# Layer 0 alone: stores issued by ScalarE, x by group in one transfer, and six rows in the first chunk of values

## The chip, the cores and the metric

The kernel runs on one core of a Trainium2 chip. Its time is the device time in microseconds (us) of that core from the start to the end of the program. A core has a matrix engine (TensorE, PE in the profile), a vector engine (VectorE, DVE), an activation engine (ScalarE, ACT), a general engine (GpSimd, POOL) and an engine that only issues transfers (SyncE, SP). Each runs its own instructions in order, and they wait for each other through semaphores. Transfers between the main memory (DRAM) and the on-chip memory are moved by 16 DMA engines. They are started by an instruction on SP or ACT, and that engine goes on to its next instruction when the transfer has been issued, not when it has landed.

## The reference

Two layers run over x, 8 images of 256 channels and 64 x 64 pixels. Each has the form x + f(norm(x)), with a group norm over 8 neighbouring channels.

```python
# layer 0: a kernel of 3 x 3 taps made from the pixel itself (32 groups of 8 channels share it)
x1, x2, x3 = conv1x1(x, w1, b1), conv1x1(x, w2, b2), conv1x1(x, w3, b3)
h = concat([x1, unfold3(reflect_pad(x2))])
h = conv1x1(relu(bn(h)), cw1)
w = conv1x1(relu(bn(h)), cw2, cb2)           # (B, 32 groups, 9 taps, H, W)
out = einsum('bgskhw,bgkhw->bgshw', unfold3(zero_pad(x3)), w)
x = x + out
# layer 1: 7 x 7 window attention in 4 heads plus a dynamic depthwise convolution
q, k, v = c1x1(x, Wq), c1x1(x, Wk), c1x1(x, Wv)
att = softmax(q . (unfold7(reflect_pad(k)) + unfold7(pe)))
out_att = att . unfold7(reflect_pad(v))
out_conv = sum over taps of softmax(Wfc x) * dwconv(relu(dwconv(x)))
x = x + rate1 * out_att + rate2 * out_conv
```

## The kernel before

An image is cut into 8 bands of 8 rows (512 pixels), so there are 64 bands. Layer 0 runs ahead of layer 1 by 12 bands (`AHEAD = NB + 4`), and both are written into one loop over `g` from -12 to 63. The loop body has 8 steps `s`. Band `g` is done in layer 1, and the parts of layer 0 for the bands `g + 12`, `g + 11` and `g + 10` are put beside it by `beside` and `steer`. For `g < 0` there is no layer 1 yet: that stage is called alone in the code (`alone = g < 0`; for the tap weights and for the load of x by group it is `g < -1` and `g < -2`). The order on each engine is the order in which the program is written. `after(n, f)` puts a piece of work n places later, where `advance` counts six places for each step.

The parts of layer 0 for one band, in the order of their data:

- `load_x` (L99) brings x of a band in the layout channels by pixels twice, as `xs` for the statistics (L283) of an image that comes later and as `xc` for the convolutions.
- `small_maps` (L328) and `write_maps` (L343, L347) make x1 and x2, `value_maps` makes x3 in two halves of 128 channels (L369 on PE, L374 on ACT). Each half lies in `x3n` and is stored to DRAM by SP (L375), since the next part needs another layout.
- `hidden_maps` makes the hidden maps: L420 three times on ACT, L430 on PE, L437 on ACT. `tap_weights` makes the nine tap weights in three parts (L466 on PE).
- `values_by_group` loads `x3q`, x3 of a band in a layout with 32 groups times 4 quarters of the band in the partitions and 8 channels times 2 rows in each (L389, L393, L397: six transfers, and the last takes a row of the band after). `x_by_group` loads x of the band in the same layout, `xg`, as four transfers of a quarter each (L405). A run of memory in such a transfer is 2 rows of one channel, 128 elements or 512 bytes.
- `product(j)` multiplies a tap weight with x3q (L479 on DVE, 9 for a band). Alone, six of the nine products are added to xg on POOL (L487), and three are added up on PE (L500) and joined at the end on DVE (L507). `take` then makes the statistics for layer 1 (L515) and stores the band to DRAM as x1 with four transfers by SP (L519).

Layer 1 loads rows from x1 (`load_rows`, L553 to L557) and normalises them (L562). `values` makes the attention's values in chunks of 8 rows: chunk 0 of an image has the rows 3 to 7 of `yp` (its first three rows lie outside the image), the last chunk has four, and each of the others has 8. A matmul makes two rows (L592), and ACT copies them to `vc` (L600, L603). `store_values` stores a chunk to `vd` in DRAM, with three columns mirrored on each side: two transfers for the rows (L616) and, where the numbers of even and odd rows are equal, six for the mirrored columns (L621). Chunk 0 has five rows, so there the mirrored columns take twelve (L625). `mirror_rows` (L632) copies the mirrored rows, and `value_tile` loads what a tile of pixels needs (L643).

Two more orders matter. The framework gives the transfers of both issuing engines eight completion semaphores in turn, in the order of the program, so a transfer's issue also waits for the completion of the one eight before it. And buffers are in rings: `xs` has 1, `xc` 2, `xg` 3 (alone), `x3q` 2, `prod` 2, `x3n` one for each half and `vc` 1.

## Time and profile before

| | us |
|---|---|
| median of 3 runs | 3959.33 (3959.31 to 3961.93) |
| the profiled execution | 3964.1 |
| its span in the trace | 3962.3 |
| TensorE busy in it | 3794.8 |
| SP from the first to the last issue of the first chunk's edge columns (L625, 12 issues) | 7.92 |
| DMA share of queue q1 over the span (SP's transfers) | 44.9% of 16 engines |

The profiled execution is one run on its own. A difference that is worked out from its trace is taken from its own time first. In lines of the profile, `x<-x3n` is the store of x3, `x<-xg` the store of x1, `DVE L507` the addition that completes a band of layer 0 while it runs alone, and `SPq` an issue on SP, whose duration is that of the issue. A time line's row has the start, the duration, the engine, the line, the operation, output and input, and in brackets how long the engine had been idle and what ended that.

The page's 40 slices, of 99 us each, show the two stages: the first two and a half slices are layer 0 alone.

```profile
PE   5789999999999999999999999999999999999998
...
DMA  8874444544445444454445544444444544323211
```

### The profile page before, as it was taken

The numbers are of one execution on the slowest core, as the hardware profiler recorded it, in microseconds if no ns is written. First come the engines' busy times: TensorE is split into PE (matmuls) and PEld (weight loads), VectorE is DVE, ScalarE is ACT, GpSimd is POOL, SyncE is SP. The second block draws the span as 40 slices with busy tenths as digits, with TensorE's granted clock in tenths as the row PEclk, the third lists the DMA queues.
The fourth block names the chain that finished last, engine by engine and source line by source line (L and its number), as shares of the span: only waits on it lengthen the run. The fifth ranks groups of instructions, "written<-read, shape, count | busy, mean of one in ns | idle before, by whom it ended". The sixth has DMA issues, their size and how long they took to land.

```text
span 3962.3 us, 71885 instructions
## 1 busy us (share of the span) xinstructions
PE 3794.8 (96%) x24620; PEld 2110.4 (53%) x24620; DVE 3418.4 (86%) x7143; ACT 2839.8 (72%) x6779; POOL 3174.4 (80%) x2156
## 2 busy tenths in 40 slices
PE   5789999999999999999999999999999999999998
PEld 2345555555555555555555555555555555555554
DVE  5768988888988988888988988988988889978778
ACT  3457777777777777777777777777777777677776
POOL 4758988888987988978888888978988888966665
PEclk9999999999999999999999999999999999999999
DMA  8874444544445444454445544444444544323211
GB/s 227 194 184 115 123 119 114 134 125 123 119 109 144 123 122 109 118 142 125 119 111 129 131 123 122 111 135 127 117 112 104 127 116 107 86 69 92 71 60 34
DMA packets 489711, 472.80 MB, mean 119 GB/s; under 512 B 64208, under 2 KB 390400, under 8 KB 489088
## 3 DMA queue, kind: packets, MB, share of 16 engines
q1 hardware_dynamic: 486016, 463.66, 44.9%
q8 instruction: 194, 3.18, 0.3%
q10 hardware_dynamic: 3328, 4.55, 0.3%
q14 instruction: 173, 1.42, 0.1%
HBM read 329.08 MB, written 142.43 MB: 119 GB/s over the span
## 4 chain that ended last, share of the span: by engine, by line
PE 33%; POOL 26%; DVE 19%; ACT 9%; issue 6%; DMA 4%; SPq 3%; POOLq 0%; DVEq 0%; ACTq 0%
PE pf L872 15%; POOL xg L487 13%; POOL ex L1081 6%; DVE prod L479 4%; DVE rec L893 4%; DVE acc L855 4%; PE small L785 3%; ACT x L343 3%; PE sco L736 3%; PE ptp L773 2%; PE pq L671 2%; PE pk L692 2%; ACT ex L877 2%; POOL tot L888 2%; PE pv L592 2%
## 5 line engine op out<-in xcount | busy, mean ns | idle before, releaser
L872 PE MATMUL pf<-yp,c_wfc 128*128 128x512 f32 x4096 | 1909.2, 595 | 17.3 <-ACT ex L877 15.0
L487 POOL TENSOR_TENSOR xg<-xg,prod 128x1024 f32<-128x1024 f32 x549 | 1200.6, 2187 | 145.4 <-DVE prod L479 108.8
L872 PEld LDWEIGHTS pf<-yp,c_wfc 128*128 128x128 f32 x4096 | 740.2, 190 | 742.0 <-issue 644.0
L1081 POOL TENSOR_TENSOR ex<-ex,ex 128x1024 f32<-128x1024 f32 x384 | 907.8, 2364 | 53.9 <-ACT ex L877 49.8
L479 DVE SCALAR_TENSOR_TENSOR prod<-pw,c_par,x3q 128x1040 f32<-128x1040 f32 x576 | 737.5, 1287 | 137.1 <-PE pw L466 66.2
L829 DVE SCALAR_TENSOR_TENSOR acc<-yp,c_chan,acc 128x504 f32<-128x504 f32 (+3 forms) x1104 | 774.7, 702 | 41.0 <-ACT acc L820 20.6
L855 DVE SCALAR_TENSOR_TENSOR acc<-hid,c_chan,acc 128x504 f32<-128x504 f32 (+3 forms) x1024 | 749.4, 732 | 20.1 <-ACT acc L849 1.9
L877 ACT ACTIVATE ex<-pf 128x512 f32<-128x512 f32 x1024 | 602.4, 588 | 199.7 <-PE pf L872 184.7
L758 ACT ACTIVATE prob<-prob,nmax 128x196 f32<-128x196 f32 x1024 | 459.1, 451 | 210.7 <-DVE nmax L750 210.4
L767 ACT ACTIVATE prob<-prob,tot 128x196 f32<-128x196 f32 x1024 | 413.0, 452 | 231.4 <-DVE tot L765 230.5
L894 POOL TENSOR_TENSOR tot<-tot,rec 128x256 f32<-128x256 f32 x254 | 185.3, 729 | 402.7 <-DVE rec L893 386.1
L893 DVE RECIPROCAL rec<-tot 128x256 f32<-128x256 f32 x256 | 445.8, 1741 | 10.6 <-POOL tot L888 5.2
L775 ACT COPY pt<-ptp 112x512 f32<-112x512 f32 x511 | 294.8, 577 | 114.7 <-PE ptp L773 113.6
L750 DVE CUSTOM_DVE_ANT_0 prob<-sco,c_mask 128x196 f32<-128x196 f32 x1024 | 324.2, 354 | 22.1 <-PE sco L736 22.0
L773 PEld LDWEIGHTS ptp<-ident,prob 128*112 128x112 f32 x2044 | 226.3, 133 | 188.6 <-issue 136.2
L773 PE MATMUL ptp<-ident,prob 128*112 128x128 f32 x2044 | 320.4, 279 | 1.3 <-ACT vc L600 1.3
L785 PEld LDWEIGHTS small<-pt,vt 112*64 112x64 f32 x8144 | 258.8, 138 | 79.1 <-issue 75.7
L785 PE MATMUL small<-pt,vt 112*64 112x64 f32 x8144 | 295.1, 225 | 2.1 <-DMA vt<-vd 1.7
L736 PE MATMUL sco<-kb,qb 64*64 64x196 f32 x4096 | 235.9, 343 | 35.5 <-DVE kb L707 32.7
L592 PE MATMUL pv<-c_wv,yp 128*128 128x256 f32 (+1 forms) x1056 | 253.8, 383 | 7.2 <-ACT yp L562 6.0
L369 PE MATMUL p<-xc,w3s 128*128 128x512 f32 x512 | 247.6, 607 | 7.0 <-ACT ex L877 7.0
L888 POOL TENSOR_SCALAR tot<-tot 128x512 f32<-128x512 f32 x127 | 243.6, 1918 | 11.1
(139 smaller groups left out, 4689.5 us busy)
## 6 DMA issues: line engine op xcount, KB each, us to landing
vt<-vd SPq DMA_DIRECT2D x512, 112.0 KB
x<-x3n SPq DMA_DIRECT2D x128, 264.0 KB
x3q<-x SPq DMA_DIRECT2D x128, 264.0 KB
xc<-in_x SPq DMA_DIRECT2D x64, 512.0 KB
xg<-in_x SPq DMA_DIRECT2D x256, 128.0 KB
x<-xg SPq DMA_DIRECT2D x256, 128.0 KB
yp<-x SPq DMA_DIRECT2D x128, 256.0 KB
xr<-x SPq DMA_DIRECT2D x64, 512.0 KB
```

Source lines behind the costliest of these rows:

```text
L479: nc.vector.scalar_tensor_tensor(prod[:, :, :RUN], pw[:, j, :RUN].unsqueeze(1).to_broadcast([P, SHARE, RUN]), par[:, PCB2 + k : PCB2 + k + 1],
L487: nc.gpsimd.tensor_add(im.xg[i], im.xg[i], rows(prod))
L758: nc.scalar.activation(prob[:, h, :NKEY], prob[:, h, :NKEY], AF.Exp, bias=nmax[:, h : h + 1], scale=-1.0, accum_out=tot[:, h : h + 1],)
L767: nc.scalar.activation(prob[:, h, :NKEY], prob[:, h, :NKEY], AF.Copy, scale=tot[:, h : h + 1])
L773: nc.tensor.transpose(ptp[:, h, ch], prob[:, h, ch * CHUNK : (ch + 1) * CHUNK], ident)
L785: nc.tensor.matmul(po[half[h], :, t * TQ : (t + 1) * TQ], im.vt[i + ch, m][:n, t, (2 * ct + h) * HD : (2 * ct + h + 1) * HD], pt[:n, h, ch ...
L829: nc.vector.scalar_tensor_tensor(o, yp[:, ct, ra + dr : rb + dr, ca + dc : cb + dc], chan[:, ct, CW1 + k : CW1 + k + 1], o, ALU.mult, ALU.add,
L855: nc.vector.scalar_tensor_tensor(o, hid[:, ra + dr : rb + dr, ca + dc : cb + dc], chan[:, ct, CW2 + k : CW2 + k + 1], o, ALU.mult, ALU.add,)
L872: nc.tensor.matmul(pf, wfc[:, kt, 2 * m + j, ct * P : (ct + 1) * P], images[b].yp[i][:, kt, PAD : PAD + R], start=(kt == 0), stop=(kt == N ...
L877: nc.scalar.activation(ex[:, j].rearrange("p (r c) -> p r c", r=R), pf, AF.Exp)
L893: nc.vector.reciprocal(rec, v)
L1081: after(4, lambda ex=ex, exb=exb: nc.gpsimd.tensor_add(ex, ex, exb))
```

## The change

Three things are changed.

While layer 0 is alone, `value_maps` has its store of x3 issued by ScalarE, and `take` has the four stores of x1 issued by ScalarE nine places later (`keep`). Beside layer 1 both stay with SP.

The host lays out x a second time, by image and band in the layout of `xg`, so that a partition's 8 channels times 2 rows are one run of 1024 elements. `x_by_group` loads it with one transfer in place of four, for all 64 bands.

The first chunk of values has six rows, 3 to 8, in place of five. Row 8 is also the first row of the chunk after it. The numbers of even and odd rows are then equal in every chunk, so `store_values` has one form with six transfers for the mirrored columns, `values` one form with whole matmuls of two rows, and `vd` one row more.

```diff
-    def value_maps(b, i, mt):
+    def value_maps(b, i, mt, alone):
...
-        nc.sync.dma_start(out=im.x3[i][mt * P : (mt + 1) * P], in_=x3n[mt])
+        queue = nc.scalar if alone else nc.sync
+        queue.dma_start(out=im.x3[i][mt * P : (mt + 1) * P], in_=x3n[mt])
...
-        for q in range(NQR):
-            nc.sync.dma_start(
-                out=t[q * REL : (q + 1) * REL].rearrange("p s r c -> p s (r c)"), in_=pieces(x_in[b][:, i * BAND : (i + 1) * BAND], q)
-            )
+        nc.sync.dma_start(out=t.rearrange("p s r c -> p (s r c)"), in_=ins["xg"][b, i])
...
-            t = im.x1[i] = dram.tile([C, BAND], F32, tag="x1", name=f"x1_{b}_{i}")
+            im.x1[i] = dram.tile([C, BAND], F32, tag="x1", name=f"x1_{b}_{i}")
+            if alone:
+                after(9, lambda: keep(nc.scalar))
+            else:
+                keep(nc.sync)
+
+        def keep(queue):
             for q in range(NQR):
-                v = x[q * REL : (q + 1) * REL].rearrange("p s r c -> p s (r c)")
-                nc.sync.dma_start(out=pieces(t, q), in_=v)
+                v = im.xg[i][q * REL : (q + 1) * REL].rearrange("p s r c -> p s (r c)")
+                queue.dma_start(out=pieces(im.x1[i], q), in_=v)
...
-        first, last = (PAD, R) if j == 0 else (0, R) if j < NB else (R - 1, R + PAD)
+        first, last = (PAD, R + 1) if j == 0 else (0, R) if j < NB else (R - 1, R + PAD)
...
-            n = min(2, last - r) * W
-            if n <= 0:
+            if r >= last:
                 break
...
-                    pv[:n, g], yp[:, kt, r : r + n // W].rearrange("p r c -> p (r c)"), wv[:, kt],
+                    pv[:, g], yp[:, kt, r : r + 2].rearrange("p r c -> p (r c)"), wv[:, kt],
...
-        vd = im.vd[j] = dram.tile([R, WP, C], F32, tag="v", name=f"vd_{b}_{j}")
+        vd = im.vd[j] = dram.tile([R + 1, WP, C], F32, tag="v", name=f"vd_{b}_{j}")
...
-        count = [(last - first + 1 - p) // 2 for p in range(2)]
+        count = (last - first) // 2
...
-                if count[0] == count[1]:
-                    o = vd[at : at + 2 * count[0], to].rearrange("(u p) n -> p u n", p=2)
-                    nc.sync.dma_start(out=o, in_=vc[c : c + W + 1 : W, : count[0]])
-                else:
-                    for p in range(2):
-                        o = vd[at + p : at + p + 2 * count[p] - 1 : 2, to : to + 1].rearrange("u c n -> c u n")
-                        nc.sync.dma_start(out=o, in_=vc[p * W + c : p * W + c + 1, : count[p]])
+                o = vd[at : at + 2 * count, to].rearrange("(u p) n -> p u n", p=2)
+                nc.sync.dma_start(out=o, in_=vc[c : c + W + 1 : W, :count])
...
+    quarters = arr["x"].reshape(-1, REL, SHARE, NB, NQR, PIECE)
+    arr["xg"] = quarters.transpose(0, 3, 4, 1, 2, 5).reshape(-1, NB, P, SHARE * PIECE)
```

More of the change, by code (lines that the diff above doesn't have):

```diff
@@ L584, in values @@
         pv = ps.tile([P, 2, C], F32, tag="gen", name=f"pv_{b}_{j}_{half}", bufs=4)
-        done = []
         for g in range(2):
             r = first + 4 * half + 2 * g
-            n = min(2, last - r) * W
-            if n <= 0:
+            if r >= last:
                 break
@@ L592, in values @@
                 nc.tensor.matmul(
-                    pv[:n, g], yp[:, kt, r : r + n // W].rearrange("p r c -> p (r c)"), wv[:, kt],
+                    pv[:, g], yp[:, kt, r : r + 2].rearrange("p r c -> p (r c)"), wv[:, kt],
                     start=(kt == 0), stop=(kt == NCT - 1),
                 )
-            done.append(n)
+            n = g + 1
         def take():
-            if len(set(done)) == 1:
-                nc.scalar.copy(vc[: done[0], 2 * half : 2 * half + len(done)], pv[: done[0], : len(done)])
-            else:
-                for g, n in enumerate(done):
-                    nc.scalar.copy(vc[:n, 2 * half + g], pv[:n, g])
+            nc.scalar.copy(vc[:, 2 * half : 2 * half + n], pv[:, :n])
         return take
@@ L610, in store_values @@
         vc = im.vc[j]
-        vd = im.vd[j] = dram.tile([R, WP, C], F32, tag="v", name=f"vd_{b}_{j}")
+        vd = im.vd[j] = dram.tile([R + 1, WP, C], F32, tag="v", name=f"vd_{b}_{j}")
         first, last, at = value_rows(j)
-        count = [(last - first + 1 - p) // 2 for p in range(2)]
+        count = (last - first) // 2
         for p in range(2):
-            to = vd[at + p : at + p + 2 * count[p] - 1 : 2, PAD : PAD + W]
-            nc.sync.dma_start(out=to.rearrange("u c n -> c u n"), in_=vc[p * W : (p + 1) * W, : count[p]])
+            to = vd[at + p : at + p + 2 * count - 1 : 2, PAD : PAD + W]
+            nc.sync.dma_start(out=to.rearrange("u c n -> c u n"), in_=vc[p * W : (p + 1) * W, :count])
         for d in range(1, PAD + 1):
             for to, c in ((PAD - d, d), (PAD + W - 1 + d, W - 1 - d)):
-                if count[0] == count[1]:
-                    o = vd[at : at + 2 * count[0], to].rearrange("(u p) n -> p u n", p=2)
-                    nc.sync.dma_start(out=o, in_=vc[c : c + W + 1 : W, : count[0]])
-                else:
-                    for p in range(2):
-                        o = vd[at + p : at + p + 2 * count[p] - 1 : 2, to : to + 1].rearrange("u c n -> c u n")
-                        nc.sync.dma_start(out=o, in_=vc[p * W + c : p * W + c + 1, : count[p]])
+                o = vd[at : at + 2 * count, to].rearrange("(u p) n -> p u n", p=2)
+                nc.sync.dma_start(out=o, in_=vc[c : c + W + 1 : W, :count])
     def mirror_rows(b, j):
@@ L965, in beside @@
             if s == (2 if alone else 0):
-                (mid if alone else end).append(lambda: value_maps(bq_, iq, 0))
+                (mid if alone else end).append(lambda: value_maps(bq_, iq, 0, alone))
             if s == (3 if alone else 1):
-                mid.append(lambda: value_maps(bq_, iq, 1))
+                mid.append(lambda: value_maps(bq_, iq, 1, alone))
         if 0 <= g + AHEAD - 1 < B * NB and s == (2 if alone else 1):
```

## Prediction

> **What bounds the kernel now.** I read the page's busy times and 40 slices first, then a table of stretches, then the chain of waits of one short window, then each engine's own time line in that window.

> ```profile
> PE 3794.8 (96%) x24620; PEld 2110.4 (53%) x24620; DVE 3418.4 (86%) x7143; ACT 2839.8 (72%) x6779; POOL 3174.4 (80%) x2156
> ```

> ```profile
> 71.00:228.00 157.00, 122.69 (x591) 59.95 (x589) 125.06 (x140) 63.91 (x119) 114.14 (x88) 0.91 0.85 197
> 228.00:300.00 72.00, 60.10 (x301) 32.90 (x302) 44.61 (x93) 40.82 (x90) 37.51 (x22) 0.91 0.67 165
> 300.00:3900.00 3600.00, 3525.26 (x23204) 1972.09 (x23203) 3164.96 (x6734) 2670.13 (x6417) 2965.62 (x1995) 1.00 0.44 114
> ```

> In the table (stretch, its length, busy us of PE, PEld, DVE, ACT, POOL, TensorE clock, DMA share, GB/s) PE is busy 97.9% of 300 to 3900 us. That stage is TensorE's; a transfer that gets cheaper there is worth nothing. From 71 to 228 us, layer 0 alone, no engine is full: DVE 80%, PE 78%, POOL 73%, ACT 41%, the DMA engines 85%. What holds it is a chain. One band (from one L507, the addition that completes a band, to the next) reads:

> ```profile
> 129.10 1.22 DVE xg L507
> ...
> 132.28 0.61 SPq L519
> ...
> 133.64 0.43 SPq L375
> ...
> 136.22 0.61 SPq L405
> ...
> 139.47 6.39 DMA x3q<-x
> ...
> 145.98 0.15 DVE prod L479
> ...
> 147.79 1.09 DVE xg L507
> ```

> The time lines of SP, of DVE and of POOL around that window:

> ```profile
> 130.34 2.55 SPq L519 DMA_DIRECT2D x<-xg  x4
> 132.93 0.61 SPq L99 DMA_DIRECT2D xs<-in_x  x1
> 133.64 0.43 SPq L375 DMA_DIRECT2D x<-x3n  x1
> 134.12 2.71 SPq L405 DMA_DIRECT2D xg<-in_x  x4
> ...
> 140.12 0.61 SPq L397 DMA_DIRECT2D x3q<-x  x1
> ```

> ```profile
> 142.90 1.27 DVE L283 BATCH_NORM_STATS2 st<-xs 128x6 f32<-128x512 f32 x2
> 145.98 1.30 DVE L479 SCALAR_TENSOR_TENSOR prod<-pw,c_par,x3q 128x1040 f32<-128x1040 f32 x1 [1.81 <-DMA x3q<-x]
> ```

> ```profile
> 114.64 11.21 POOL L487 TENSOR_TENSOR xg<-xg,prod 128x1024 f32<-128x1024 f32 x5 [2.76 <-DVE prod L479]
> 134.19 11.21 POOL L487 TENSOR_TENSOR xg<-xg,prod 128x1024 f32<-128x1024 f32 x5 [2.76 <-DVE prod L479]
> ```

> A loop closes through SP: L507 releases the four x1 stores (2.55 us), behind them stand xs, the second x3n store, four xg loads (2.71) and six x3q loads (4 us); the last x3q is issued 11.0 us after L507 and lands 5.7 us later; then one product (1.3), and the next L507. Yet the x3n store was ready early: its activation ended at 128.5, its issue came at 133.64. Only queue order ties x3q to L507.

> [...] In 90.85 to 109.56 us stretches of 2 KB rows (xs) move 370 to 390 GB/s, those of 512 B to 1 KB (xg, x3q) 190 to 250[...] Here 0.61 us of issue against 5.7 us until DVE starts, so I count both.

> **The change part by part.**

> *Stores on ScalarE.* In a band SP issues 18 transfers; six leave (two x3n 0.34 to 0.43 us, four x1 0.61 to 0.64: 3.3 us) and go to ACT. ACT is busy 8 us of a 19.5 us band. Behind them on ACT stands the third hidden activation (L420), which before waits for PE's L430: at 115.90 us, 6.3 us after L507. The x1 stores, placed nine steps later, would be issued 2 to 4.7 us after L507: hidden, with 1.6 us to spare. If that cover is gone each us costs a us of the band, since hidden, L466 and the last three products follow.

> *One load for xg.* Three issues fewer on SP (3 x 0.65 = 2.0 us). 0.52 MB at 200 GB/s is 2.6 us of the DMA engines, at 380 GB/s 1.4: 1.2 us less of 16.9 per band (90% of 18.71). The run of 4 KB is in no trace before; bounds are 0 (no quicker) and 2 us.

> *What then ends a band.* x3q no longer queues behind L507. The built program keeps one tie: DMAs of both queues take eight completion semaphores in turn, and each waits for the one eight before it. So the fourth x3q piece of a band waits until a first x1 store landed, in most bands. Its store issues about 2 us after L507, lands about 4 us later, then two issues (1.3): last issue near 7 us instead of 11. Landing near 13; the product can start at about 14.5, when DVE is through. x3q then is just in time, and POOL's fifth addition ends the band (134.19 + 11.21 = 145.40, where L507 came at 147.71). How much earlier than L507 it ended before, band by band (L507 at 90.85, 109.56, 129.10, 147.71, 167.65, 187.81, 205.63): 0.6, 2.4, 3.2, 1.7 (0.6 for L231 taken off), 0, 3.2, 0. At 227.62 DVE waited 4.47 for x3q and its L466 was done at 220.8: 4.3. Sum 15.4 us. Cycles shorter by this ask the DMA engines for 15.7 of some 16.5 us, so some landing will still be late: I take 85%, **13.1 us**; bounds 5 (x3q stays late) and 19 (all, plus less of the slow TensorE clock).

> *The start.* x3q of band 0 landed at 54.5 with its issues from 46.25. With one xg load and no stores ahead, issues begin near 42.7, but the last waits for the second store of band 1, and on ACT that store waits for xg of band 0 (semaphore again): about 2.5 us of ACT stalled. I take **2 us** gained, bounds 0 and 3.5.

> *Six rows in the first chunk.* TensorE has the same number of matmuls (128 columns of weights for 64), ACT the same copies. SP issues two stores and six edge stores instead of two and twelve. In the middle of an image's work that is hidden by PE. At 239.69 to 248.97 us it is not: twelve L625 take 7.92, and behind them SP issues xr, x3q, the mirror rows, the next chunk's stores and at 261.62 the xs for which DVE waits 8.33 us, to 265.3, while PE idles. Six issues of 0.66 are 4.0; SP enters 0.5 earlier because its x1 and x3n issues are gone: **4.4 us**, bounds 2 (vc's second copy, which waits for L592 at 249.2, holds the queue) and 6. The wider row adds 64 KB of store, 0.3 us of the DMA engines at 200 GB/s, under the same issues.

> *After 300 us.* 52 bands load xg with three issues less: hidden by PE, nothing, bounds -3 to +3.

> Sum: 13.1 + 2 + 4.4 = 19.5, taken as 20. The profiled execution took 3964.1 (span 3962.3 and 1.8 around it): 3944. It stands 4.8 above the median of 3959.33, so against that: **3939 us**.

> **The rivals.**

> *The tie holds (3950).* The eight semaphores keep x3q behind the x1 stores, now behind their landing. For: the last x3q issue still follows L507 by a landing. Against: the 4 us of landing are less than the 9.8 us of SP issues they replace. Then a third of 15.4 remains (5), with 4.4 of the transition: 3959.3 - 9.6.

> *More than the sum (3927).* The bands with 0 gain had a granted TensorE clock of 0.73 and 0.83 where busier ones had 0.9 to 1.0; with fewer waits they may come up to those: 1.5 us a band over eight bands, 12 us.

> *Nothing (3959).* Stage two starts earlier, but something in it was waiting anyway. Against: PE is at 97.9% from the first 50 us on.

> *Slower (3971): ScalarE is held at its stores.* ACT runs in order. The third x1 store waits for the landing of the first x3n store, the fourth for xs or xg. With landings of 4 us this costs nothing; it decides from about 6 us, when L420 is late. If landings take 8.5 under 95% DMA load, each of eight bands loses 2.1 instead of gaining, 17 us, the start loses 0 and the transition still gains 4.4: 3959.3 + 12. For: x3q takes 5.7 now. Against: that is 0.66 MB with xg's packets before it.

> **How the numbers follow.** Forecast 0.62, tie 0.17, more 0.10, nothing 0.04, slower 0.07. The forecast's own bounds (7 to 28 gained) give 3931 to 3952. The range 3922 to 3955 takes in "more" and most of the tie, and leaves out about 0.2. A measurement of this kernel tells 0.2% (8 us) from no change: the tie splits over that bound, so faster 0.82, same 0.11, slower 0.07.

> **What would show it.** L507 to L507 near 16.4 us where it was 18.6 to 20; DVE's waits on x3q (11.6 us of 57 to 230 by name, and 6.3 more put down to PE and POOL) mostly gone, POOL's waits on products smaller; xs of the transition issued within 18 us of the first vd store, not 22; from 300 us on the same durations, shifted. It is wrong if L420 starts over 8 us after L507, if x3q's last issue is still 10 us after it, or if the stage after 300 us changes length by over 4 us.

## The result and the profile after

| | before | after |
|---|---|---|
| median, us | 3959.33 (5 runs, 3957.30 to 3962.34) | 3945.96 (5 runs, 3937.60 to 3947.43) |
| ratio | | 0.9960, 95% interval 0.9948 to 0.9972 |
| the profiled execution, us | 3964.1 | 3947.27 |
| a second measurement, median, us | 3961.49 (15 runs) | 3940.01 (4 runs), ratio 0.9951 (0.9936 to 0.9966) |

The changed kernel is 13.4 us faster in the first measurement and 21.5 in the second; 20 were forecast. Lines have moved a little: L507 is now L505, L479 is L477, L487 is L485, L420 is L418, L430 is L428, L466 is L464, L519 is L523, L625 is L618.

A table of stretches of the changed kernel (stretch, length, busy us of PE, PEld, DVE, ACT, POOL with counts, TensorE clock, DMA share, GB/s), cut at its nine L505 additions, so that each line is one band:

```profile
68.38:86.93 18.55, 15.18 (x72) 7.72 (x71) 16.89 (x16) 7.27 (x13) 13.76 (x11) 0.91 0.70 201
86.93:103.27 16.34, 14.04 (x74) 6.89 (x73) 14.69 (x14) 8.25 (x16) 13.77 (x11) 1.00 0.84 229
103.27:120.58 17.31, 13.48 (x68) 7.02 (x67) 14.66 (x14) 6.67 (x12) 13.74 (x11) 0.90 0.78 205
120.58:139.66 19.08, 15.94 (x71) 7.87 (x70) 15.23 (x18) 7.65 (x15) 13.89 (x11) 0.82 0.80 214
139.66:163.12 23.46, 20.34 (x92) 11.06 (x91) 16.38 (x27) 9.60 (x21) 13.99 (x12) 0.78 0.64 177
...
196.78:218.70 21.92, 18.56 (x76) 9.65 (x74) 17.57 (x26) 8.70 (x16) 15.06 (x15) 0.77 0.86 254
```

Before, these bands took 19.15, 18.71, 19.54, 18.61, 19.94, 20.16, 17.82 and 21.99 us, 155.9 in all; now 150.3. One reaches the 16.4 us of the forecast (16.34). One, of 23.46 us, is longer than any was before. The column of the clock shows where: the longest bands have the lowest clock. Stretches in which TensorE was granted half its clock were there before too: from 62 to 240 us they last 34.1 us before and 41.0 us now.

The largest of DVE's waits from 71 to 219 us, before and after, in order of size (us in total, times, longest):

```profile
DVE prod L479 <- DMA x3q<-x: 7.1, 3, 4.0
DVE prod L479 <- PE pw L466: 6.2, 3, 3.0
```

```profile
DVE prod L477 <- PE pw L464: 7.6, 4, 3.3
DVE prod L477 <- POOL xg L485: 4.2, 4, 1.4
```

x3q was the largest entry and is gone. The tap weights from TensorE were second and now lead. The time line of ScalarE in the third of the bands above, then the chain of waits over the same stretch, show what the tap weights waited for there:

```profile
104.14 0.33 ACTq L376 DMA_DIRECT2D x<-x3n  x1
...
106.64 0.33 ACTq L376 DMA_DIRECT2D x<-x3n  x1
107.06 4.11 ACTq L523 DMA_DIRECT2D x<-xg  x4
111.27 0.81 ACT L418 ACTIVATE hid<-x,bn1b,bn1s 96x512 f32<-96x512 f32 x1 [4.66 <-DMA x<-xg]
```

```profile
104.14 5.78 DMA x<-x3n
...
109.95 0.56 ACTq L523
...
111.27 0.82 ACT hid L418
...
112.14 0.65 PE ph L428 x8
```

Four x1 stores take 2.57 us of issue in the band before this one; here they took 4.11, because the third waited until the x3 store of 104.14 had landed, 5.78 us later: the trace counts both on completion semaphore 107, whose last update for the x3 store came at 109.93, and the issue followed at 109.95. (All 2638 transfers in this trace are counted on eight such semaphores. In the trace of before, 2846 of the 2854 that SP issues after its first eight are on that of the one eight before.) L418 stands behind them, and TensorE's L428 behind L418.

In the transition, SP's queue and the statistics that waited for xs (idle time in brackets):

```profile
228.78 1.30 SPq L614 DMA_DIRECT2D vd<-vc  x2
230.13 3.24 SPq L618 DMA_DIRECT2D vd<-vc  x6
...
245.33 0.39 SPq L99 DMA_DIRECT2D xs<-in_x  x1
```

```profile
248.90 1.29 DVE L283 BATCH_NORM_STATS2 st<-xs 128x6 f32<-128x512 f32 x2 [3.10 <-DMA xs<-in_x]
```

From the first vd store to xs it is 16.6 us where it was 21.9. From 248.90 to the end of the span it is 3696.6 us, before (from 265.30) 3697.0: all that the change brought lies ahead of this point.

### The profile page after: what moved, and what is told of

The parts are those of the page before. It is cut to its first block, busy times and chain, and to the rows that moved or that the text cites. A ratio compares the mean times of both kernels' runs of the same rounds, so it can differ in the third digit from the quotient of the medians.

```text
span 3945.5 us, 71644 instructions
## 1 busy us (share of the span) xinstructions
PE 3790.7 (96%) x24620; PEld 2115.6 (54%) x24620; DVE 3418.8 (87%) x7143; ACT 2843.1 (72%) x6779; POOL 3174.3 (80%) x2156
## 4 chain that ended last, share of the span: by engine, by line
POOL 31%; PE 30%; DVE 20%; ACT 9%; issue 7%; DMA 3%; SPq 0%; ACTq 0%; POOLq 0%; DVEq 0%
POOL xg L485 16%; PE pf L865 14%; POOL ex L1074 7%; DVE prod L477 5%; DVE acc L848 4%; DVE rec L886 4%; ACT x L343 3%; PE small L778 3%; PE sco L729 2%; PE ptp L766 2%; ACT ex L870 2%; PE pk L685 2%; PE pq L664 2%; DMA x<-x3n 2%; POOL tot L881 2%
## 5 line engine op out<-in xcount | busy, mean ns | idle before, releaser
L865 PE MATMUL pf<-yp,c_wfc 128*128 128x512 f32 x4096 | 1906.4, 594 | 16.8 <-ACT ex L870 11.7
L485 POOL TENSOR_TENSOR xg<-xg,prod 128x1024 f32<-128x1024 f32 x549 | 1201.0, 2188 | 126.0 <-DVE prod L477 90.9
L477 DVE SCALAR_TENSOR_TENSOR prod<-pw,c_par,x3q 128x1040 f32<-128x1040 f32 x576 | 737.7, 1287 | 117.1 <-PE pw L464 63.4
L886 DVE RECIPROCAL rec<-tot 128x256 f32<-128x256 f32 x256 | 445.8, 1741 | 12.6 <-POOL tot L881 7.6
L729 PE MATMUL sco<-kb,qb 64*64 64x196 f32 x4096 | 235.6, 343 | 34.1 <-DVE kb L700 32.7
L464 PEld LDWEIGHTS pw<-h2n,c_c 128*128 128x128 f32 x1152 | 177.4, 195 | 145.1 <-issue 120.1
L664 PE MATMUL pq<-yp,c_wq 128*128 128x512 f32 x512 | 242.7, 596 | 12.0 <-ACT ex L870 12.0
L369 PE MATMUL p<-xc,w3s 128*128 128x512 f32 x512 | 247.5, 607 | 7.0 <-ACT ex L870 7.0
```

Source lines behind the costliest of these rows:

```text
L477: nc.vector.scalar_tensor_tensor(prod[:, :, :RUN], pw[:, j, :RUN].unsqueeze(1).to_broadcast([P, SHARE, RUN]), par[:, PCB2 + k : PCB2 + k + 1],
L485: nc.gpsimd.tensor_add(im.xg[i], im.xg[i], rows(prod))
L865: nc.tensor.matmul(pf, wfc[:, kt, 2 * m + j, ct * P : (ct + 1) * P], images[b].yp[i][:, kt, PAD : PAD + R], start=(kt == 0), stop=(kt == N ...
L886: nc.vector.reciprocal(rec, v)
```

## The experiments

Two theories for what the bands did not give. **Hold**: ScalarE is held at x1's stores by landings, L418 is late, and so is the band. **Clock**: TensorE loses half its clock after a stretch in which it idles (in the first profile the granted clock was 0.50 from 129.2 to 136.0 us, behind 3.41 us of which TensorE was busy for 1.26), and a wait that POOL's chain would cover turns into lost time only then. Three numbers of a profile tell them apart: the sum of the eight bands, the start of L418 (here always the third of a band, the one behind x1's stores) after the addition that begins the band, and the time at half clock between 62 and 240 us (twice the missing clock).

**One part at a time.** *act_only* has the stores on ScalarE alone, *xg_only* the single load, *rows_only* the six rows; each is the diff above cut to that part. (The additions counted in the expectation as second to tenth are the first to ninth.)

> Only the stores move to ScalarE; xg keeps four loads, the first chunk five rows. Between the stores of x1 and what was issued before them stand xg's four loads now, so the third and fourth x1 store wait for a landing of xg. If ScalarE's hold at its stores is what took back the gain (theory 'hold'): L421 (the third hidden activation) starts over 8 us after the addition that completes a band, the eight cycles from the second to the tenth addition sum to 150 to 156 us (before 155.9, all three changes 150.3), and the time is 3952 to 3960. If SP's queue was the whole matter (theory 'queue', which takes the x3q issues off the x1 stores): cycles near 145, time near 3948.

> Only the load of x by group becomes one transfer; all stores stay on SP. SP issues three transfers less in front of x3q in each band (2.0 us). Theory 'queue': in the bands where DVE waited for x3q this is worth up to 2 us, eight bands, less where POOL or PE is late next: the eight cycles fall by 6 to 12 us, the transition by 0 to 1, time 3947 to 3953. Theory 'the stores matter, the load does not' (the last x3q issue is still behind x1's stores and the second x3 store): under 3 us, 3956 to 3960.

> Only the first chunk of values gets six rows. Six issues of 0.66 us leave the front of the xs that DVE waits for in the transition. Own effect as the prediction costed it: 4.0 us, so 3955, with xs issued 18 us after the first vd store where it was 22. If the 7.5 us that the transition gained with all three changes come from this edit alone: 3952. If it needs the other two (a queue that is there earlier): under 2 us, 3957 to 3960.

| | median | ratio to before (3960.33, 49 runs) | eight bands | last addition to L283 at about 300 us |
|---|---|---|---|---|
| before | | | 155.9 | 97.4 |
| act_only | 3958.55 (13 runs) | 0.9994 (0.9985 to 1.0002) | 145.6 | 99.5 |
| xg_only | 3956.39 (21 runs) | 0.9989 (0.9982 to 0.9995) | 145.4 | 94.9 |
| rows_only | 3955.02 (21 runs) | 0.9986 (0.9980 to 0.9993) | 156.2 | 91.5 |

act_only cannot be told from before. Its bands are 10 us shorter, as 'queue' said of them, but the time that 'queue' forecast was missed by 10 us and lies in the range of 'hold'. Its first addition comes at 75.88 in place of 71.70 (TensorE waits 9.0 us at once for a hidden activation, and is at half clock for 13.7 us from 43 to 57), and the transition is 2 us longer. Its profiled execution was the slowest of its 13. xg_only fell between its two theories: its bands are 10.5 us shorter, as 'queue' said, and its median is 3.9 us lower, in the range of the other. Its profile (3949.71) is the fastest of its 21, with 14.2 us at half clock where before has 34.1, so its bands flatter it. rows_only did what was forecast and more: 5.3 us, and xs issued 16.5 us after the first vd store. In all three the last column holds 10.2 us at half clock (before has 13.7), so with as much half-clock time rows_only stands 8.0 and 3.4 us under the others. The three sum to 11.0 us; together they gave 13.4 and 21.5.

**The hold taken away.** *late*: all three changes, x1's stores behind L418 and L435 on ScalarE.

```diff
-                after(9, lambda: keep(nc.scalar))
+                after(20, lambda: keep(nc.scalar))
```

> All three changes, but x1's stores come 20 places after the band's completion in place of 9, so that on ScalarE they stand behind the third hidden activation L418 and behind L435, in front of five idle us, and no x3q piece waits for them. Theory 'hold': L418 starts at most 7.5 us after L505 where it was 8 to 9.4, PE's waits on hid fall from 23.8 to under 14 us, cycles 3 and 4 fall from 17.3 and 19.1 to about 16.5 to 17, the eight cycles from 150.3 to 140 to 145, time 3937 to 3941 against 3946. Theory 'clock' (the cycles of 23.5 and 21.9 us are long because TensorE's granted clock was 0.50 for 8 to 10 us in each, whoever waits): L418 is early, but long cycles with a clock under 0.85 remain and the eight sum to 147 or more, time 3944 to 3948.

It took 3937.52 us (3935.00 to 3939.88; ratio 0.9943, 0.9930 to 0.9955). The interval overlaps those of the changed kernel, but all five executions are under 3940 us, three of nine of the changed kernel's are. Three of its bands by the same table:

```profile
102.53:118.88 16.35, 13.52 (x73) 6.66 (x72) 14.70 (x15) 7.75 (x15) 13.77 (x11) 1.00 0.83 233
118.88:135.24 16.36, 13.13 (x67) 5.91 (x66) 15.20 (x17) 7.77 (x15) 13.77 (x11) 1.00 0.85 226
135.24:153.81 18.57, 15.73 (x88) 8.45 (x89) 16.39 (x27) 7.93 (x18) 14.10 (x12) 0.91 0.75 213
```

L418 starts 6.3 us after the addition in six of the eight bands, TensorE's waits on hid from 71 to 219 us are 7.3 us against 15.4, and the bands sum to 137.9. 'Hold' forecast the time. But half-clock time fell too, from 41.0 to 10.2 us (20.5 in *late_xs* and *late_edge* below, which leave x1's stores at the same place), so this run alone does not tell the theories apart.

**The changed kernel once more**, *after_again*.

> The changed kernel once more, for a second profile. Theory 'hold': in the bands from 71 to 219 us L418 starts 7.3 to 9.4 us after L505 again and PE's waits on hid are 18 us or more, since the semaphores that hold x1's stores are those of the program. Theory 'clock': the long cycles (19.1, 23.5 and 21.9 us) come where TensorE was granted 0.50, and in another execution they lie elsewhere or are gone; the span moves by the difference, and the part from the first xs statistics of the full stage (L283) to the end is 3696 to 3697 us as in the six profiles so far. Time 3937 to 3948 in both.

```profile
102.38:118.72 16.34, 13.91 (x73) 6.78 (x71) 14.80 (x15) 8.20 (x15) 13.76 (x11) 1.00 0.90 236
118.72:135.06 16.34, 13.53 (x72) 6.51 (x70) 15.20 (x16) 8.07 (x15) 13.75 (x11) 1.00 0.88 230
135.06:156.16 21.10, 18.48 (x88) 10.35 (x89) 16.38 (x26) 8.10 (x18) 14.10 (x12) 0.76 0.62 180
```

The program is the same, and L418 starts 6.3 to 8.2 us after the addition, not up to 9.4: the hold varies from one execution to the next. TensorE's waits on hid from 71 to 219 us are 11.0 us (15.4 in the first profile), where 'hold' forecast 18 or more. The bands that took 17.31 and 19.08 us take 16.34 each at full clock, with L418 at 7.3 and 6.8 us where it was at 8.0 and 8.7. The eight sum to 143.3, half-clock time is 30.7, and the execution 3940.48: 6.8 us under the first profile, of which the bands are 7.0. A half-clock stretch by itself need not lengthen a band: the band before these (86.01 to 102.38, not shown) took 16.37 with TensorE at half clock from 90 to 94 us, ahead of L418, which started at 8.0. In the first profile the stretches came behind it, at 112 to 116 and 129 to 136 us, when the tap weights were due.

**TensorE kept busy, the hold left in place.** *fill* and *fill_half* add matmuls of no use, four and two a band, where TensorE waits for the held L418; *late_fill* adds four to *late*.

```diff
+            def fill():
+                t = small_tile(f"fill_{b}_{i}")
+                for _ in range(4):
+                    nc.tensor.matmul(t[:, :BAND], ident[:96], hids[1][:96].rearrange("p r c -> p (r c)"), start=True, stop=True)
+
+            after(12, fill)
             after(12, lambda: after(4, lambda ph=conv(home, 2, 3, 0, 2): relu(ph)))
```

> The changed kernel as it is, with x1's stores in front of L418, and four matmuls of no use (96 x 128 by 512 columns, into a PSUM tile that is free then) put in every band of layer 0 alone between the first 16 and the last 8 matmuls of L428, where TensorE idles 2.3 us for the held L418. The hold is not touched. So far half-clock stretches came in multiples of 3.41 us and after stretches with TensorE under 60% busy: 30.7 and 41.0 us of them in 62 to 240 us in the two profiles of the changed kernel, 10.2 in 'late'. Theory 'clock' (idle TensorE loses its clock, and a hold that POOL's chain would cover turns into lost time only then): under 15 us at half clock, the eight cycles sum to 136 to 141 us, time 3936 to 3940 with little scatter. Theory 'hold alone': nothing gained, the 1.9 us of added matmuls show: cycles 17 to 19 us, time 3945 or more.

> 'late' with the same four matmuls. There L418 is not held, TensorE has less idle time at that place and was at half clock for 10.2 us only. Theory 'clock': half-clock time falls further, 3934 to 3938. If the added matmuls themselves are on the path (L428, L464 and the last three products follow them): L418's successors late by up to 1.9 us a band, time 3940 to 3950.

> As 'fill' with two added matmuls in place of four: 3.7 us of them filled more than the 2.3 us hole, and TensorE itself then set the band at 17.46 us, without half-clock time from 62 to 240 us. Two take 1.85 us, less than the hole, so TensorE has some 15.9 us of work in a band of 16.4. Theory 'clock': half-clock time under 10 us in 62 to 240, cycles of 16.4 to 17 with the hold of L418 in place, the eight sum to 136 to 141 us, time 3937 to 3941 in a scatter of under 5 us. Theory 'hold alone' (or half-clock stretches come back because 1.85 us isn't enough): cycles over 17.3 in bands where L418 starts over 8 us after the addition, time 3942 to 3948.

fill took 3946.99 us, late_fill 3948.36. The four matmuls take 3.70 us, in the trace eight of 0.46, twice the 1.9 us reckoned (L369's matmuls of 512 columns took 30.7 us for 65 before, from 71 to 228 us, 0.47 each), and TensorE sets the band itself:

```profile
113.15 0.65 PE L428 MATMUL ph<-hid,c_c 128*32 128x128 f32 x16
113.73 3.70 PE L458 MATMUL small_fill<-hid,ident 96*128 96x512 f32 x8
117.36 0.42 PE L428 MATMUL ph<-hid,c_c 96*32 96x128 f32 x8
```

So the time was missed. But half-clock time went to 0.0 (late_fill 3.4). Three bands of fill take 17.45 to 17.48 us with L418 at 7.4 to 8.2 us after the addition, four of late_fill 17.45 to 17.47 with L418 at 6.3: under TensorE's own limit such a hold doesn't show. Two of fill with L418 at 9.4 and 9.5 take 18.16 and 17.86, at full clock: a hold as long as that does.

fill_half took 3939.97 us (3937.90 to 3946.72), half-clock time 10.2, eight bands 141.3; its scatter of 8.8 us is wider than expected. Of two neighbouring bands

```profile
88.20:105.57 17.37, 15.35 (x69) 6.86 (x68) 14.67 (x14) 6.81 (x13) 13.77 (x11) 0.90 0.75 206
105.57:121.92 16.35, 15.27 (x76) 7.31 (x75) 14.70 (x15) 7.83 (x15) 13.76 (x11) 1.00 0.84 230
```

both have L418 at 7.9 us after the addition, and only the one with a half-clock stretch is longer. That 1.0 us is not the hold's: the stretch lies ahead of L418, at the same place as in the band of after_again that lost nothing, and here the two added matmuls, which it made late, ran until 98.17 us, 1.2 us past the end of L418, with L428's last eight behind them. Of the hold the other band speaks: L418 at 7.9 us, full clock, 16.35. That the added matmuls save time in the whole kernel isn't shown: 3939.97 lies within the changed kernel's own scatter.

**Where else x1's stores can stand.** *early* puts them 2 places after the addition, still in front of L418 and free of this band's x3 landings; *late_sp* is *late* with `keep(nc.sync)`.

> All three changes, but x1's stores come 2 places after the band's completion in place of 9. They stand in front of L418 on ScalarE as in the changed kernel, with the same issues (4 x 0.64 us), but each follows eight transfers that were issued before this band's x3 stores, so none waits for one of them to land. Theory 'hold by the landing': L418 starts at most 7 us after L505, the eight cycles sum to 138 to 144 us, time 3937 to 3941. Theory 'ScalarE's time for four issues itself': L418 stays 8 to 9 us after L505, cycles 17 to 19, time 3944 to 3948.

> As 'late', but SP issues x1's stores, 20 places after the band's completion, that is behind x3q; ScalarE keeps the x3 stores. If x3q's place in SP's queue is what mattered and ScalarE isn't needed for x1: cycles 16.4 to 17, time 3937 to 3942 as 'late'. If x1's stores, which wait for L505, hold back the next band's xc, xs and xg behind them on SP: xs or xc waits appear (DVE on xs, PE on xc), cycles over 18, time 3948 or more.

early: 3943.76 us, between its theories. Its stores take 2.6 us in five of eight bands, so hardly a landing holds them; but they now push all three hidden activations back (the third 7.1 to 9.7 us after the addition). The second to fifth band take 17.1 to 17.6 us, and the eight 139.9. In the second, third and fourth a half-clock stretch begins 8.5 to 8.7 us after the addition, right behind L418, so issue time and clock are not apart there. late_sp: 3952.83 us (ratio 0.9975, 0.9966 to 0.9984), the time of the second theory. The largest of SP's waits from 71 to 219 us:

```profile
SPq L99 <- DMA x<-x3n: 27.9, 5, 9.3
SPq L390 <- DMA x<-x3n: 22.6, 5, 7.4
SPq L405 <- DMA x<-x3n: 15.7, 4, 4.3
```

The signs that the second theory gave did not show: no wait of DVE on xs and none of PE on xc is listed. SP stands at the loads of the next band for the landing of the x3 stores, and x3q behind them is late again: in the third band, at full clock and with L418 at 6.3, the last piece is issued 13.2 us after the addition (9.0 in late), and the band takes 18.44. That it is x1's stores that bring SP into these waits is argued, not shown.

**What hold and clock do together.** The second, third, fourth, sixth and seventh band of seven profiles, in us, with the start of L418 after the addition in brackets; + marks a half-clock stretch that begins when L418 starts or after it (8.5 us or more after the addition), - one that begins ahead of it. The first band takes 18.55 to 18.57 us in six of the seven whatever L418 and the clock do, and the fifth and the eighth hold other work too; they are left out.

| | second | third | fourth | sixth | seventh |
|---|---|---|---|---|---|
| after | 16.34 (7.3) | 17.31 (8.0) + | 19.08 (8.7) + | 16.94 (7.6) | 16.72 (6.3) |
| after_again | 16.36 (8.0) - | 16.34 (7.3) | 16.35 (6.8) | 16.96 (7.6) + | 17.21 (7.9) + |
| early | 17.24 (7.9) + | 17.08 (7.8) + | 17.55 (7.8) + | 16.95 (8.3) | 16.71 (7.9) |
| late | 16.37 (6.3) | 16.35 (6.3) | 16.36 (6.3) | 16.93 (6.3) | 16.70 (6.3) |
| late_xs | 16.39 (6.3) | 16.35 (8.0) - | 16.38 (6.3) | 16.98 (6.3) | 16.70 (6.3) |
| late_edge | 16.36 (6.3) | 16.35 (8.0) - | 16.33 (6.3) | 16.95 (6.3) | 16.71 (6.3) |
| fill_half | 17.37 (7.9) - | 16.35 (7.9) | 16.35 (7.6) | 16.96 (8.6) | 16.71 (7.2) |

Without a + a band has the same length within 0.06 us, whether L418 starts 6.3 or 8.6 us after the addition; the exception is the band of fill_half above. The sixth of late and of fill_half:

```profile
153.81:170.74 16.93, 15.87 (x81) 8.06 (x80) 14.79 (x15) 9.28 (x17) 14.04 (x10) 1.00 0.75 208
156.63:173.59 16.96, 15.20 (x75) 7.27 (x75) 14.70 (x16) 7.78 (x15) 14.19 (x11) 1.00 0.76 217
```

With a + six of seven bands are longer, by 0.5 to 2.7 us. And the hold brings the stretches: of the ten in the eight bands of after and after_again, seven begin in a wait of TensorE for L418 of 1.6 to 3.1 us or within 0.7 us behind it. Of the nine in late, late_xs and late_edge none does; TensorE's waits for L418 near them are 0.8 us or less. So in these profiles, up to about 8.6 us, the hold costs through the clock that TensorE loses over it, not by itself. Neither theory was right alone. One point stays open: no band of the table has a + with L418 at 6.3 us, so what such a stretch costs without the hold is not shown. And part of the stretches come with other waits, those of the kernel before (34.1 us) among them.

**The transition.** *late_xs* issues the xs of the last pass in front of the vd stores, *late_edge* gives the first chunk's six edge stores to ScalarE.

```diff
-        if s == (3 if g < -1 else 7) and g + AHEAD0 < B * NB:
-            first_stats(*divmod(g + AHEAD0, NB), n=40 if g < -1 else 9)
+        if s == (3 if g < 0 else 7) and g + AHEAD0 < B * NB:
+            first_stats(*divmod(g + AHEAD0, NB), n=40 if g < -1 else 33 if g < 0 else 9)
```

```diff
+        queue = nc.scalar if b == j == 0 else nc.sync
...
-                nc.sync.dma_start(out=o, in_=vc[c : c + W + 1 : W, :count])
+                queue.dma_start(out=o, in_=vc[c : c + W + 1 : W, :count])
```

> As 'late', and in the last pass before layer 1 the load of xs for the statistics is issued four steps earlier (step 3 in place of 7), in front of the vd stores; its statistics stay in their place. In 'late' DVE waits 6.49 us for this xs at 239.6 us, behind ten vd issues on SP, and PE idles. If SP's order in front of xs bounds the transition: that wait is gone, time 3 to 6 us under 'late', 3932 to 3935. If something else is late next there (the product's tap weights, x3q, POOL's additions): under 2 us, 3936 to 3938.

> 'late' with the six edge-column stores of the very first chunk of values issued by ScalarE in place of SP, so that SP's queue from 217 to 256 us is six issues (3.3 us) shorter. If SP's whole queue bounds the transition (moving xs forward in it gained nothing): 2 to 4 us under 'late', 3934 to 3936. If ScalarE is held at them as it was at x1's stores (they wait for semaphores of loads of yp), qb's L668 and L435 behind them come late: 3937 to 3942.

3938.95 and 3938.23 us: neither median beats late's. In late_xs DVE's wait of 6.49 us for xs is gone, and nothing is gained; SP then runs on without a pause, to the loads of values (L636):

```profile
233.42 3.85 SPq L618 DMA_DIRECT2D vd<-vc  x6
237.37 2.59 SPq L523 DMA_DIRECT2D x<-xg  x4
240.01 8.75 SPq L636 DMA_DIRECT2D vt<-vd  x12
```

In late_edge SP reaches xr 3.6 us earlier, but the second chunk's vd store is at 230.21 us (229.73 in late) and xs at 235.49 (235.76). So this xs was the wait that showed, not the bound, and what holds the second chunk's stores there is left open. From the last addition to the statistics at about 300 us the profiles read 93.1 us (late), 92.6 (late_xs) and 90.9 (late_edge). The last has 3.4 us less at half clock, and its five executions spread over 7.7 us, so a gain of up to 2 us from it is neither shown nor excluded.

## Why the prediction was right

Direction and range held. By its own steps:

- *Start, 2 us.* The first addition moved from 71.70 to 68.38 (67.46 in after_again): 3.3 to 4.2. Not all of this is the change's: rows_only, which leaves the start as it was, has it at 69.30.
- *Bands, 13.1 us.* 5.6 in the first profile (155.9 to 150.3), 12.6 in the second. This is the term that was mis-sized in the measurement on record. Three inputs failed. "Hidden, with 1.6 us to spare" took stores issued 2 to 4.7 us after the addition and landings of 4 us (an estimate; in the trace of before, from 71 to 228 us, x3's stores land in 2.05 to 4.90 us, median 4.2, and x1's in 2.36 to 2.65); in the third band above they ran from 3.8 to 7.9 us, behind a landing of 5.78. "If that cover is gone each us costs a us of the band" failed as well: with TensorE at full clock L418 came up to 2.2 us later than 6.3 at no cost. And the clock stood in the sum only as an upside ("more than the sum"), where the waits that the hold brings to TensorE cost it the clock, as in seven of the ten stretches counted above. The saving of the long rows of xg is not isolated: from 71 to 219 us the DMA engines moved 192 GB/s at 84% busy before and 213 at 85% in xg_only, but also 203 at 79% in act_only, which has the short rows.
- *Transition, 4.4 us.* 7.4 and 7.1 us between the last addition and the statistics at 300 us. rows_only alone gives 6.0 (97.4 to 91.5): twelve issues in 7.92 us became six in 3.26, where six of 0.66 were reckoned. That xs is the work to be waited for was wrong as a mechanism: late_xs took that wait away for nothing.
- *After 300 us, nothing.* The part behind is 3636.8 us, before 3637.3.
- The sum, 20, stands against 16.8 and 23.6 between profiled executions, and 13.4 and 21.5 between medians. In the first profile it came near by luck in part: bands that gave 7.5 us too little stand against a start and a transition that gave 4.3 too much.

The rival "slower: ScalarE is held" named the right mechanism and the right store, and set its turning point at landings of about 6 us. At landings of 5.8 us (third band of the first profile) and 5.1 us (fourth) part of the gain went, as the clock fell behind the hold. "The tie holds" is true of the issue: in the first five bands the last x3q came 8.2 to 10.4 us after the addition, not 7. (By the waits from 71 to 219 us SP stood at the x3q loads L390 and L398 for 42.5 us until x3 stores landed, and for 3.8 us until x1 stores did.) It cost nothing, since DVE no longer waits for it. The signs given for being right showed (bands of 16.3 us in one profile or the other, x3q's waits gone, xs after 16.6 us, the rest unchanged), but two given for being wrong showed too and were badly chosen: L418 over 8 us after the addition in four of eight bands (two of eight before the change), and a last x3q 10 us after it in three of the first five. Neither says whether a later engine waits. "More than the sum" (3927) was not reached: the fastest median of all kernels here is 3937.5, with the stores put elsewhere, and the changed kernel's fastest execution comes to 3937.6.

## What to carry over

A store moved to a compute engine stands in that engine's order with its waits for earlier transfers, not only its issue time (x1's four took 4.11 us in the third band, 2.57 in the second): put it in front of that engine's longest idle time, behind the work others wait for (*late* has x1's there, at 3937.52 us). A wait that another chain covers isn't free where TensorE's clock falls behind it (six of seven bands with such a stretch were 0.5 to 2.7 us longer): read the clock column band by band, and take more than one profile, before a gain is spread evenly over bands. And a wait that ends last by the view of waits is only a candidate for the bound until something behind it is seen to move.

## What the runs showed of the hardware

```profile
122.33:125.75 3.42, 3.42 (x11) 1.51 (x11) 3.42 (x5) 2.57 (x4) 1.87 (x2) 1.00 1.04 283
125.75:129.16 3.41, 1.26 (x18) 0.38 (x16) 3.41 (x3) 0.00 (x0) 3.33 (x2) 1.00 0.60 174
129.16:132.57 3.41, 2.42 (x15) 2.02 (x16) 0.10 (x2) 1.27 (x2) 3.14 (x2) 0.51 0.95 227
132.57:135.99 3.42, 3.42 (x6) 0.90 (x6) 3.42 (x3) 0.00 (x0) 2.03 (x1) 0.50 1.07 240
135.99:139.40 3.41, 3.41 (x19) 1.90 (x18) 2.91 (x5) 2.28 (x5) 2.33 (x2) 0.99 0.26 83
```

TensorE was busy 1.26 of 3.41 us in the second cell, in which it waits for the held L418, and ran the next two at half clock. Over the six profiles, from 36 us on for 60 cells each, 308 cells at full clock have a next one: after 31 of them the clock fell, and in 28 of these TensorE had been busy under half of the time by the profile (in the other three 0.55, 0.55 and 0.77); where it stayed full, the lowest busy share was 0.43 to 0.45, by how finely the cells are cut. Of 31 half-clock cells that a full one followed, all were busy 0.88 or more. The clock fell behind cells that were not idle, too: the second above was busy for 0.37 of its length. What the changed kernel meets differs with the execution: of the two profiles, half-clock time from 62 to 240 us is 41.0 us in one and 30.7 in the other. The changed kernel's nine executions spread over 10 us, and their mean granted clock goes with it: the five of 3937.6 to 3940.6 us had 0.994 or 0.995, the four of 3946.0 to 3947.6 us 0.992 or 0.993. Of the two that were profiled, 6.8 us apart, everything behind the xs statistics (248.90 and 242.28 us) is the same within 0.2 us.
